# Packing the closing products of an attention-convolution kernel: 32 channels of o under c2's 96 rows, the other 64 as half pieces

## The chip, the cores and the metric

The kernel runs on one core of a Trainium2 chip. The time is the device time of one execution in microseconds (us); lower is better. Engines are named as in the profile: PE is TensorE's matmul queue and PEld its weight loads, DVE is VectorE, ACT is ScalarE, POOL is GpSimd, SP is SyncE, which here issues most DMAs.

## The reference, cut to what matters

Two layers work on x of 4 images, 96 channels, 128 x 128 pixels, float32. Layer 0 is a group norm, a projection with a depthwise convolution, a four-direction state-space scan and an output projection. Layer 1 is what matters here:

```python
xr, x1, x2 = _relu_split_norm(x, sc1, sc2, res_coef, nc1, nc2)
y1 = NORM_SCALE * _layer_norm(_attn_conv(x1, x2, aw1, aw2, aw3))
y2 = NORM_SCALE * _layer_norm(_conv2d(x2, w_conv2, K // 2)) * x1
y = jnp.concatenate([y1, y2], axis=1)
return xr + _conv2d(y, w_full, 0) + b_full[None, :, None, None]
```

`_attn_conv` convolves with weights that each image makes for itself by a softmax. Its output is called o below, and the convolution `_conv2d(x2, w_conv2)` is called c2. The last line is a 1 x 1 convolution over 2 x 96 channels: 96 of y1 and 96 of y2. The layer norms take one mean and one variance for a whole image. The kernel folds them in: o's scale `ro` goes into the weights, o's mean becomes a constant for each output channel, and c2 has its mean subtracted before it is multiplied by x1. `xr`, the residual, is piecewise linear in x with one slope and offset above a threshold and another below.

## The kernel before

The kernel is one instruction stream made by Python generators. `co_run(left, right, pace)` draws from two generators in turn; each `yield` tells how much time of the other side the piece is worth. After the scan of layer 0 (it ends near 3.4 ms), `left` is `attend` of image b: the image's convolutions by a product scheme with separate planes of pixels, first the two maps (c2 among them) and then the attention convolution that makes o. `light` is a chain of side work for the neighbouring images: `norm` and `split` of image b+1, then `close` of image b-1. A scheduler sets the final order of the instructions on every engine, and each engine then works through its queue in order.

Close is `attn_output`. It runs for images 0, 1 and 2, each time beside the attention of a later image. The last image is closed by another class, `LastOutput`, which uses `own_weights`, `c2_weights` and `residual` too but whose tile loop is not touched by the change.

Before its loop Close makes two weight matrices. `own_weights` (L2267 to L2274) makes `w1`: 96 rows of the 1 x 1 weights of o times `ro`, and a 97th row with the constants: `low`'s offset for each channel, less mean times weights, made by two small products (L2271, L2272). `c2_weights` makes `w2` (L2256). `with_ones` (L2278) makes two buffers for o whose 97th row is one, so that the product of `w1` with o adds the constant.

The loop goes over 16 tiles of 1024 pixels. For each tile:

- SP loads o, c2 and xx (the layer's input) of the next tile, 96 partitions x 4 KB each (L2312, L2315).
- `first_half`: ScalarE makes a linear function of xx (L2283) and VectorE masks it to x1 (L2284).
- VectorE subtracts c2's mean and multiplies by x1 (L2326), in place in `c2`.
- `residual`: ScalarE makes the upper branch's difference (L2288), VectorE masks it (L2289) and adds slope times xx (L2290).
- PE makes two results of 512 columns, one bank each, from two products each: `w1` with o (L2334), `w2` with c2 (L2335).
- VectorE adds the residual from `e` and evicts to `x1` (L2337 for image 0, whose maps have plain pixel order; L2339 for the others, which also reorders pixels).
- SP stores x1.

Tiles of pool `f3` have two buffers, and the bank pool of this side, `psr`, has two banks, so that at most one tile's results are open.

`ssm_output`, earlier in each image's life, has the same two-step packing for a product over 192 rows: 128 rows first (L1023), then 64 rows split in two halves of the pixels, which lie on partitions 0 to 63 and 64 to 127 (L1028).

Of the kernel before, what the change touches and what calls it, by code (L numbers as in the profile page):

```python
# [9 lines left out]
F32 = mybir.dt.float32  # L10
BF16 = mybir.dt.bfloat16
AF = mybir.ActivationFunctionType
ALU = mybir.AluOpType
# [4 lines left out]
C = 96  # L18
H = W = 128
L = H * W  # L20
CH = 512
# [32 lines left out]
SN = 1024  # L54
# [17 lines left out]
def kernel(  # L72
# [26 lines left out]
    nc = tc.nc  # L99
# [6 lines left out]
    def load(src, name):  # L106
        t = const.tile(list(src.shape), F32, name=name, tag=name)
        nc.sync.dma_start(t, src)
        return t
# [44 lines left out]
    def filled(value, name, n=C, p=C):  # L154
        t = const.tile([p, n], F32, name=name, tag=name)
        nc.vector.memset(t, value)
        return t

    mean96 = filled(1.0 / C, "mean96")
# [17 lines left out]
    def col(name, width=1, bufs=None):  # L177
        return small.tile([C, width], F32, name=name, tag=name, bufs=bufs)

    def rsqrt(dst, var):  # L180

        t = col("rsq")
        nc.vector.tensor_scalar(t, var, GN_EPS, None, ALU.add)
        nc.scalar.activation(t, t, AF.Sqrt)
        nc.vector.reciprocal(dst, t)

    def combine(ps, stats, mat, name, mv=None):


        if mv is None:  # L190
            mv = small.tile([stats.shape[0], 2], F32, name="mv", tag=f"mv{stats.shape[0]}")
            nc.vector.bn_aggr(mv, stats)  # L192
        n = mv.shape[0]
        p1 = bank(ps)[:n, 0:2]
        nc.tensor.matmul(p1, lhsT=mat, rhs=mv, start=True, stop=True)  # L195
        r = small.tile([n, 2], F32, name=name, tag=name)
        nc.vector.tensor_copy(r, p1)
        d2 = small.tile([n, 1], F32, name=f"d2{n}", tag=f"d2{n}")
        nc.vector.tensor_sub(d2, mv[:, 0:1], r[:, 0:1])
        nc.vector.tensor_mul(d2, d2, d2)  # L200
        p2 = bank(ps)[:n, 0:2]
        nc.tensor.matmul(p2[:, 0:1], lhsT=mat, rhs=d2, start=True, stop=True)  # L202
        nc.vector.tensor_add(r[:, 1:2], r[:, 1:2], p2[:, 0:1])
        return r, mv
# [84 lines left out]
    def bank(ps):  # L289

        return ps.tile([128, CH], F32, name="bank", tag="bank")

    def part(ps, *shape):
        n = 1
        for d in shape[1:]:
            n *= d
        t = bank(ps)[: shape[0], :n]
        return t if len(shape) == 2 else t.rearrange("p (a b) -> p a b", b=shape[2])
# [1922 lines left out]
            yield from lift(H)  # L2221
            later.flush()

    def c2_weights(img, ps, pool):


        n = NSTRIP
        mva, mvb = (pool.tile([128, 2], F32, name=f"mv_{i}") for i in "ab")
        for mv, st, p, e, k in (
            (mva, img.c2a, 96, 128, 4 * n - img.mapped),  # L2230
            (mvb, img.c2b, 0, 64, 2 * n - (not img.mapped)),
            (mvb, img.c2b, 64, 128, 2 * n - 1),
        ):
            v = st[p:e, :k].rearrange("p c s -> p (c s)")
            nc.vector.bn_aggr(mv[p:e], v)
        halves = ((mva[96:128], m96[96:128]), (mvb, mrows[img.mapped]))

        def over(n):
            pt = bank(ps)[:, 0:n]
            for i, (mv, mat) in enumerate(halves):  # L2240
                nc.tensor.matmul(
                    pt, lhsT=mat, rhs=mv[:, 0:n], start=(i == 0), stop=(i == 1)
                )
            return pt

        s2 = pool.tile([128, 2], F32, name="s2")
        nc.vector.tensor_copy(s2, over(2))
        for mv, p in ((mva, 96), (mvb, 0)):
            d = mv[p:128, 0:1]
            nc.vector.tensor_sub(d, d, s2[p:128, 0:1])  # L2250
            nc.vector.tensor_mul(d, d, d)
        nc.vector.tensor_add(s2[:, 1:2], s2[:, 1:2], over(1))
        r2 = col("r2")
        rsqrt(r2, s2[0:C, 1:2])
        w2 = pool.tile([C, C], F32, name="w2")
        nc.vector.tensor_scalar(w2, wful[:, 1], r2, None, ALU.mult)  # L2256
        return s2, w2

    def own_weights(img, ps, pool):

        so, _ = combine(ps, img.ost.rearrange("p c s -> p (c s)"), mean96, "so")
        ro = col("ro")
        rsqrt(ro, so[:, 1:2])
        w1 = pool.tile([128, C], F32, name="w1")
        nc.vector.tensor_scalar(w1[0:C], wful[:, 0], ro, None, ALU.mult)  # L2267
        nso = col("nso")
        nc.vector.tensor_scalar(nso, so[:, 0:1], -1.0, None, ALU.mult)
        pt = bank(ps)[C : C + 1, 0:C]  # L2270
        nc.tensor.matmul(pt, lhsT=img.keep["low"][:, 1:2], rhs=ident, start=True, stop=False)  # L2271
        nc.tensor.matmul(pt, lhsT=nso, rhs=w1[0:C], start=False, stop=True)  # L2272
        nc.vector.tensor_copy(w1[C : C + 1], pt)
        return w1[0 : C + 1]  # L2274

    def with_ones(pool, name, bufs=None):
        y = pool.tile([128, SN], F32, name=name, tag=name, bufs=bufs)
        nc.gpsimd.memset(y[C : C + 1], 1.0)  # L2278
        return y[0 : C + 1]

    def first_half(img, xx, x1):
        thr, scale, shift = (img.keep[n] for n in ("thr", "scale", "shift"))
        nc.scalar.activation(x1, xx, AF.Identity, scale=scale[:, 0:1], bias=shift[:, 0:1])  # L2283
        nc.vector.scalar_tensor_tensor(x1, xx, thr, x1, ALU.is_gt, ALU.mult)  # L2284

    def residual(img, xx, e):
        up, low, thr = (img.keep[n] for n in ("up", "low", "thr"))
        nc.scalar.activation(e, xx, AF.Identity, scale=up[:, 0:1], bias=up[:, 1:2])  # L2288
        nc.vector.scalar_tensor_tensor(e, xx, thr, e, ALU.is_gt, ALU.mult)  # L2289
        nc.vector.scalar_tensor_tensor(e, xx, low[:, 0:1], e, ALU.mult, ALU.add)  # L2290

    def pixels(v):

        return v.rearrange("p (h j t) -> p h t j", j=TW, t=TN)

    def plain(v):
        return v.rearrange("p (h t j) -> p h t j", j=TW, t=TN)

    def attn_output(img, ps, side, share):
        ob = out[img.b].rearrange("c h w -> c (h w)")  # L2300
        with (
            tc.tile_pool(name="f1", bufs=1, side=side) as p1,
            tc.tile_pool(name="f3", bufs=2, side=side) as p3,
        ):
            w1 = own_weights(img, ps, p1)
            s2, w2 = c2_weights(img, ps, p1)
            ones = [with_ones(p1, f"o{i}") for i in range(2)]

            def loads(t):
                o = ones[t % 2]  # L2310
                got = [o]
                nc.sync.dma_start(o[0:C], img.od[:, bass.ts(t, SN)])  # L2312
                for name, src in (("c2", img.c2d), ("xx", img.xnew)):
                    y = p3.tile([C, SN], F32, name=name)
                    nc.sync.dma_start(y, src[:, bass.ts(t, SN)])  # L2315
                    got.append(y)
                return got

            ahead = loads(0)
            for t in range(NS):  # L2320
                o, c2, xx = ahead
                if t + 1 < NS:
                    ahead = loads(t + 1)
                x1 = p3.tile([C, SN], F32, name="x1")
                first_half(img, xx, x1)
                nc.vector.scalar_tensor_tensor(  # L2326
                    c2, c2, s2[0:C, 0:1], x1, ALU.subtract, ALU.mult
                )
                e = p3.tile([C, SN], F32, name="e")
                residual(img, xx, e)  # L2330
                for h in range(2):
                    sl = bass.ts(h, CH)
                    pf = part(ps, C, CH)
                    nc.tensor.matmul(pf, lhsT=w1, rhs=o[:, sl], start=True, stop=False)  # L2334
                    nc.tensor.matmul(pf, lhsT=w2, rhs=c2[:, sl], start=False, stop=True)  # L2335
                    if img.mapped:
                        nc.vector.tensor_add(x1[:, sl], pf, e[:, sl])  # L2337
                    else:
                        nc.vector.tensor_add(plain(x1[:, sl]), pixels(pf), pixels(e[:, sl]))  # L2339
                    yield 2.6 * share  # L2340
                nc.sync.dma_start(ob[:, bass.ts(t, SN)], x1)

# [103 lines left out]
    class Image:  # L2446
# [44 lines left out]
        def close(self, ps, side, share=1.0):  # L2491
            while not self.finished:
                at.later.tick()
            yield from attn_output(self, ps, side, share)
# [27 lines left out]
    with tc.tile_pool(name="wp", bufs=1, side="left") as wp:  # L2522
# [7 lines left out]
        for images, pace in (([0], 0.25), ([1], 0.75), ([2, 3], 1.35)):  # L2530
            left = projections(images, weights, stats, wp, psl)
            if images[0] == 0:
# [12 lines left out]
                got = next(others)  # L2545
                while not got:
                    next(left)
                    got = next(others)
# [25 lines left out]
    wful = load(w_full, "wful")  # L2574
# [123 lines left out]
```

## Time and profile before

| what | us |
|---|---|
| median of 3 runs | 6410.42 (6406.12 to 6425.06) |
| the profiled execution | 6409.68 |
| its span, first to last instruction | 6407.8 |
| PE busy | 5253.4 (82% of the span) |
| DVE busy | 4699.9 (73%) |
| ACT busy | 3759.4 (59%) |
| POOL busy | 3238.6 (51%) |
| mean granted PE clock | 0.902 |

The page shows one execution. Busy times are shares of the whole span, averaged over stages that have different limits; what a part of the kernel costs has to be read from the stretch in which it runs. A row of a group gives line, engine, operation, tiles (out<-in), shapes and count, then busy time and mean duration, then the idle time of the engine just before and what ended it. Durations of neighbouring instructions on one engine overlap a little, so the busy time of a group, which counts overlap once, is smaller than count times mean. A float32 product of 512 columns leaves two PE records.

### The profile page before, as it was taken

To read this page: it belongs to the slowest core of one execution; us is meant where nothing else is said; L and a number is where in the kernel's file an instruction comes from. 1 tells how busy PE (TensorE), PEld (TensorE's weight loads), DVE (VectorE), ACT (ScalarE), POOL (GpSimd) and SP (SyncE) were. 2 spreads that over 40 slices of the span, in tenths; PEclk is the share of its full clock that TensorE was granted. 3 is DMA by queue.
4 is the path that set the end of the run, shared out by engine and by line. 5 is a ranking of instruction groups with operands and counts; after the bars stand their busy time and mean duration, and the time that the engine had idled before them with its cause. 6 is when DMAs were issued, how large, how long until landed. Compare 5 with 4: busy or idle time off the path is not lost. (4 is left out here: it accounts for less than half of the span.)

```text
span 6407.8 us, 76468 instructions
## 1 busy us (share of the span) xinstructions
PE 5253.4 (82%) x23264; PEld 2254.8 (35%) x23264; DVE 4699.9 (73%) x7132; ACT 3759.4 (59%) x4770; POOL 3238.6 (51%) x2476
## 2 busy tenths in 40 slices
PE   6889988987888643989988588977888877889888
PEld 2333322322222111444433234345333444345553
DVE  4247878988989768989844686468774687988767
ACT  1247767787787666777622465466644665545642
POOL 1326757978879554979822234436304365022310
PEclk9899989998999765999999799989989888999989
DMA  6766777775675766676667686665776656967668
GB/s 155 175 160 189 198 199 199 214 221 163 198 202 171 202 183 207 196 213 179 182 185 195 166 228 163 195 169 156 214 199 184 175 149 165 245 167 180 191 168 221
DMA packets 897706, 1205.30 MB, mean 188 GB/s; under 512 B 230644, under 2 KB 745642, under 8 KB 884816
## 3 DMA queue, kind: packets, MB, share of 16 engines
q1 hardware_dynamic: 866640, 1145.36, 65.5%
q0 software_dynamic: 16336, 38.51, 2.3%
q10 hardware_dynamic: 14320, 16.54, 0.9%
q8 instruction: 187, 3.06, 0.2%
q14 instruction: 223, 1.83, 0.1%
HBM read 777.82 MB, written 345.62 MB: 175 GB/s over the span
## 5 line engine op out<-in xcount | busy, mean ns | idle before, releaser
L633 PE MATMUL bank<-y,wp 128*128 128x512 f32 (+3 forms) x3584 | 1310.9, 622 | 83.8 <-DMA y<-y 41.0
L866 POOL TENSOR_TENSOR y<-y,dl 128x1024 f32<-128x1024 f32 x384 | 1058.5, 2757 | 263.0 <-DVE dl L858 240.3
L833 POOL TENSOR_TENSOR dl<-dl,u 128x1024 f32<-128x1024 f32 x384 | 1008.8, 2627 | 253.1 <-ACT dA L809 121.1
L854 DVE TENSOR_TENSOR_SCAN dA<-dA,pBC 128x512 f32<-128x512 f32 x768 | 981.6, 1278 | 30.7
L2169 PE MATMUL bank<-y,wn 128*64 128x384 f32 (+5 forms) x2408 | 680.1, 507 | 58.3 <-DMA y<-x1d 34.1
L1477 PE MATMUL two<-ya,wd 128*64 128x192 f32 (+3 forms) x2376 | 582.2, 414 | 174.0 <-ACT odd L1550 65.1
L633 PEld LDWEIGHTS bank<-y,wp 128*128 128x128 f32 (+3 forms) x3584 | 456.2, 168 | 749.3 <-issue 651.1
L858 DVE TENSOR_TENSOR dl<-dA,pBC 128x512 f32<-128x512 f32 x768 | 528.5, 688 | 255.8 <-PE pBC L747 183.8
L747 PE MATMUL pBC<-xr,wbc 60*128 60x512 bf16 (+1 forms) x1536 | 457.8, 404 | 311.5 <-DVE dA L854 239.1
L1938 ACT COPY yb<-ya 64x768 f32<-64x768 f32 (+1 forms) x660 | 537.7, 815 | 195.5 <-PE two L1477 113.8
L676 ACT ACTIVATE dl<-pd,dtb 128x512 f32<-128x512 f32 x768 | 485.5, 684 | 187.9 <-PE pd L747 171.5
L1477 PE MATMUL two<-yb,wd 128*64 128x192 f32 (+3 forms) x2376 | 559.0, 400 | 4.0 <-ACT yb L1938 4.0
L837 DVE TENSOR_TENSOR pBC<-dl,pBC 128x512 f32<-128x512 f32 x768 | 527.5, 687 | 8.8 <-POOL dl L833 7.8
L2169 PEld LDWEIGHTS bank<-y,wn 128*64 128x64 f32 (+3 forms) x2408 | 310.3, 169 | 357.2 <-issue 186.2
L809 ACT ACTIVATE dA<-dl,negA 128x1024 f32<-128x1024 f32 x384 | 420.3, 1141 | 2.3
L1477 PEld LDWEIGHTS two<-ya,wd 128*64 128x64 f32 (+1 forms) x2376 | 262.2, 165 | 370.9 <-ACT odd L1550 75.0
L676 ACT ACT_TABLE_LOAD x248 | 318.2, 1283 | 91.9 <-PE pd L747 79.7
L747 PEld LDWEIGHTS <-wbc 60*128 60x128 bf16 (+1 forms) x1536 | 103.1, 96 | 752.1 <-issue 739.3
L1477 PEld LDWEIGHTS two<-yb,wd 128*64 128x64 f32 (+1 forms) x2376 | 289.7, 167 | 150.5 <-issue 42.1
L1477 PE MATMUL two<-ya,wa 128*96 128x384 f32 (+1 forms) x528 | 231.2, 521 | 72.9 <-DMA ya<-vp 27.0
L1550 ACT COPY odd<-two 128x384 f32<-128x384 f32 (+5 forms) x176 | 115.8, 658 | 291.3 <-PE two L1492 179.1
L1406 POOL TENSOR_TENSOR pl<-x 96x256 f32<-96x256 f32 (+3 forms) x396 | 275.2, 710 | 0.0
(322 smaller groups left out, 9105.4 us busy)
## 6 DMA issues: line engine op xcount, KB each, us to landing
u<-zb SPq DMA_DIRECT2D x192, 1024.0 KB
yms<-y SPq DMA_DIRECT2D x96, 512.0 KB
xn<-xnew SPq DMA_DIRECT2D x128, 384.0 KB
ya<-vp SPq DMA_DIRECT2D x120, 336.0 KB
y<-y SPq DMA_DIRECT2D x128, 258.2 KB
zb<-z SPq DMA_DIRECT2D x64, 512.0 KB
y<-yms SPq DMA_DIRECT2D x64, 512.0 KB
ya<-x1p SPq DMA_DIRECT2D x90, 336.0 KB
```

Of the source, the lines that this page charges most:

```text
L633: nc.tensor.matmul(blocks(pz[p:e]), lhsT=ws[k][:, d, c : c + e - p], rhs=window(ys[k], at, d, n), start=(i == 0), stop=(i == len(terms) - 1),)
L676: nc.scalar.activation(dst, src, AF.Softplus, bias=bias)
L747: nc.tensor.matmul(p, lhsT=w[rows], rhs=xr[rows, at : at + CH], start=True, stop=True)
L809: nc.scalar.activation(live[m]["dA"], live[m]["dl"], AF.Exp, scale=negA[:, g % 3, k : k + 1])
L833: nc.gpsimd.tensor_mul(t, t, u_view(n))
L837: nc.vector.tensor_mul(p, live[n]["dl"][:, bass.ts(half, CH)], p)
L854: nc.vector.tensor_tensor_scan(h, h, p, init, ALU.mult, ALU.add)
L858: nc.vector.tensor_mul(live[n]["dl"][:, sl], live[n]["dA"][:, sl], live[n]["C", half])
L866: nc.gpsimd.tensor_add(v, v, t.rearrange("p (a b) -> p a b", b=W))
L1477: nc.tensor.matmul(of(to[p:e], r), lhsT=w[:, i, c : c + e - p], rhs=tiles(t[k][PAIR[i]][:, SLOT[i]], o, r), start=(k == 0), stop=False,)
L1938: nc.scalar.copy(yb[k][64 * h - 64 : 64 * h, :, :n], ya[k][0:64, :, h * TN : h * TN + n])
L2169: nc.tensor.matmul(pc[p:e, :n].rearrange("p (h w) -> p h w", w=W), lhsT=w[:, c : c + e - p], rhs=v[:, :, 0:W], start=(i == 0), stop=(i == ...
```

## The change

Close is rewritten so that its rows fill the array. Of o's 96 channels, the first 32 are loaded under c2's 96 rows, so that one product contracts 128 rows with the stacked weights `stack[:, 0]`. The other 64 channels are loaded in two pieces of 512 pixels, one on partitions 0 to 63 and one on 64 to 127, and multiplied by `stack[:, 1]`, which holds the same 64 weight rows twice. The row of ones goes. Its constant, now a column `base` from a product of one column, is the bias of a ScalarE operation that makes slope times xx plus base in its own tile `g`; VectorE adds `g` to `e`. Both banks of a tile are taken before its products. A tile has five loads in place of three. The weights `w2` are written straight into the stack and `w1`'s rows are copied into it by three DMAs on POOL's queue. `own_weights` is split, so that `LastOutput` keeps what it had.

```diff
--- before.py
+++ after.py
@@ -2221,7 +2221,7 @@
             yield from lift(H)
             later.flush()
 
-    def c2_weights(img, ps, pool):
+    def c2_weights(img, ps, pool, w2=None):
 
 
         n = NSTRIP
@@ -2252,21 +2252,24 @@
         nc.vector.tensor_add(s2[:, 1:2], s2[:, 1:2], over(1))
         r2 = col("r2")
         rsqrt(r2, s2[0:C, 1:2])
-        w2 = pool.tile([C, C], F32, name="w2")
+        if w2 is None:
+            w2 = pool.tile([C, C], F32, name="w2")
         nc.vector.tensor_scalar(w2, wful[:, 1], r2, None, ALU.mult)
         return s2, w2
 
+    def own_scale(img, ps):
+
+        so, _ = combine(ps, img.ost.rearrange("p c s -> p (c s)"), mean96, "so")
+        ro, nso = col("ro"), col("nso")
+        rsqrt(ro, so[:, 1:2])
+        nc.vector.tensor_scalar(nso, so[:, 0:1], -1.0, None, ALU.mult)
+        return ro, nso
+
     def own_weights(img, ps, pool):
 
-
-
-        so, _ = combine(ps, img.ost.rearrange("p c s -> p (c s)"), mean96, "so")
-        ro = col("ro")
-        rsqrt(ro, so[:, 1:2])
+        ro, nso = own_scale(img, ps)
         w1 = pool.tile([128, C], F32, name="w1")
         nc.vector.tensor_scalar(w1[0:C], wful[:, 0], ro, None, ALU.mult)
-        nso = col("nso")
-        nc.vector.tensor_scalar(nso, so[:, 0:1], -1.0, None, ALU.mult)
         pt = bank(ps)[C : C + 1, 0:C]
         nc.tensor.matmul(pt, lhsT=img.keep["low"][:, 1:2], rhs=ident, start=True, stop=False)
         nc.tensor.matmul(pt, lhsT=nso, rhs=w1[0:C], start=False, stop=True)
@@ -2302,41 +2305,67 @@
             tc.tile_pool(name="f1", bufs=1, side=side) as p1,
             tc.tile_pool(name="f3", bufs=2, side=side) as p3,
         ):
-            w1 = own_weights(img, ps, p1)
-            s2, w2 = c2_weights(img, ps, p1)
-            ones = [with_ones(p1, f"o{i}") for i in range(2)]
+            ro, nso = own_scale(img, ps)
+            w1 = p1.tile([C, C], F32, name="w1")
+            nc.vector.tensor_scalar(w1, wful[:, 0], ro, None, ALU.mult)
+            pt = bank(ps)[:C, 0:1]
+            nc.tensor.matmul(pt, lhsT=w1, rhs=nso, start=True, stop=True)
+            base = col("base")
+            nc.vector.tensor_add(base, pt, img.keep["low"][:, 1:2])
+            stack = p1.tile([128, 2, C], F32, name="ws")
+            s2, _ = c2_weights(img, ps, p1, stack[0:C, 0])
+            nc.gpsimd.dma_start(stack[C:128, 0], w1[0:32])
+            for h in range(2):
+                nc.gpsimd.dma_start(stack[64 * h : 64 * h + 64, 1], w1[32:C])
 
             def loads(t):
-                o = ones[t % 2]
-                got = [o]
-                nc.sync.dma_start(o[0:C], img.od[:, bass.ts(t, SN)])
-                for name, src in (("c2", img.c2d), ("xx", img.xnew)):
-                    y = p3.tile([C, SN], F32, name=name)
-                    nc.sync.dma_start(y, src[:, bass.ts(t, SN)])
-                    got.append(y)
-                return got
+                c2 = p3.tile([128, SN], F32, name="c2")
+                o = p3.tile([128, CH], F32, name="o")
+                xx = p3.tile([C, SN], F32, name="xx")
+                nc.sync.dma_start(c2[0:C], img.c2d[:, bass.ts(t, SN)])
+                nc.sync.dma_start(c2[C:128], img.od[0:32, bass.ts(t, SN)])
+                nc.sync.dma_start(xx, img.xnew[:, bass.ts(t, SN)])
+                for h in range(2):
+                    nc.sync.dma_start(
+                        o[64 * h : 64 * h + 64], img.od[32:C, bass.ts(2 * t + h, CH)]
+                    )
+                return o, c2, xx
 
             ahead = loads(0)
+            up, low, thr = (img.keep[n] for n in ("up", "low", "thr"))
             for t in range(NS):
                 o, c2, xx = ahead
                 if t + 1 < NS:
                     ahead = loads(t + 1)
                 x1 = p3.tile([C, SN], F32, name="x1")
                 first_half(img, xx, x1)
+                d = c2[0:C]
                 nc.vector.scalar_tensor_tensor(
-                    c2, c2, s2[0:C, 0:1], x1, ALU.subtract, ALU.mult
+                    d, d, s2[0:C, 0:1], x1, ALU.subtract, ALU.mult
                 )
                 e = p3.tile([C, SN], F32, name="e")
-                residual(img, xx, e)
+                nc.scalar.activation(e, xx, AF.Identity, scale=up[:, 0:1], bias=up[:, 1:2])
+                g = p3.tile([C, SN], F32, name="g")
+                nc.scalar.activation(g, xx, AF.Identity, scale=low[:, 0:1], bias=base)
+                nc.vector.scalar_tensor_tensor(e, xx, thr, e, ALU.is_gt, ALU.mult)
+                nc.vector.tensor_add(e, e, g)
+                pf = [part(ps, C, CH) for _ in range(2)]
+                for h in range(2):
+                    nc.tensor.matmul(
+                        pf[h], lhsT=stack[:, 0], rhs=c2[:, bass.ts(h, CH)],
+                        start=True, stop=False,
+                    )
+                for h in range(2):
+                    p = slice(64 * h, 64 * h + 64)
+                    nc.tensor.matmul(
+                        pf[h], lhsT=stack[p, 1], rhs=o[p], start=False, stop=True
+                    )
                 for h in range(2):
                     sl = bass.ts(h, CH)
-                    pf = part(ps, C, CH)
-                    nc.tensor.matmul(pf, lhsT=w1, rhs=o[:, sl], start=True, stop=False)
-                    nc.tensor.matmul(pf, lhsT=w2, rhs=c2[:, sl], start=False, stop=True)
                     if img.mapped:
-                        nc.vector.tensor_add(x1[:, sl], pf, e[:, sl])
+                        nc.vector.tensor_add(x1[:, sl], pf[h], e[:, sl])
                     else:
-                        nc.vector.tensor_add(plain(x1[:, sl]), pixels(pf), pixels(e[:, sl]))
+                        nc.vector.tensor_add(plain(x1[:, sl]), pixels(pf[h]), pixels(e[:, sl]))
                     yield 2.6 * share
                 nc.sync.dma_start(ob[:, bass.ts(t, SN)], x1)
 
```

In the changed program the lines are: L2287 for x1's mask, L2343 for c2's operation, L2347 and L2349 for ScalarE's two operations, L2350 and L2351 for the mask and the add, L2354 for the two products of 128 rows, L2360 for the two half products, L2366 (image 0) and L2368 for the evictions.

## The prediction

> **What bounds the kernel now.** The page's first part gives TensorE (PE) 82% of the span and VectorE (DVE) 73%. Its chain covers about 1% and settles nothing, so I went by stage. The changed function, Close, runs three times (close 0, 1, 2, for images 0 to 2). The groups by form from 4640 us on, and the starts of L2334 and L2335, put them at 4646 to 4778, 5450 to 5660 and 5660 to 5906 us. The table of stretches for these (columns: busy us of PE, PEld, DVE, ACT, POOL, then granted PE clock, DMA share, GB/s):
>
> ```profile
> core 0: us, PE busy (x) PEld busy (x) DVE busy (x) ACT busy (x) POOL busy (x), PEclk, DMA share, GB/s
> 4646.00:4778.00 132.00, 105.09 (x290) 38.45 (x287) 112.55 (x127) 50.96 (x50) 13.71 (x13) 0.82 0.70 195
> 5450.00:5605.00 155.00, 138.20 (x420) 55.58 (x419) 141.96 (x178) 83.22 (x95) 0.00 (x0) 0.97 0.92 245
> 5605.00:5660.00 55.00, 46.92 (x187) 22.55 (x186) 44.19 (x69) 21.52 (x27) 2.83 (x5) 0.87 0.61 164
> 5660.00:5906.00 246.00, 224.14 (x1269) 119.69 (x1267) 200.18 (x283) 117.02 (x142) 74.81 (x94) 0.96 0.68 177
> ```
>
> The reader is to see three different limits. Close 0 is VectorE's (112.6 of 132 us). Close 1's first 155 us are tight everywhere: DVE 92%, DMA 92% at 245 GB/s, PE 89%. Close 2 is PE's (91%, DVE 81%, DMA 68%). Then the operations concerned, with out<-in, shapes, count, busy us, mean ns and the idle time before them:
>
> ```profile
> L2335 PE MATMUL bank<-c,w 96*96 96x512 f32 x192 | 108.2, 691 | 21.7 <-DVE c L2326 18.7 <-issue 2.7
> L2334 PE MATMUL bank<-o,w 97*96 97x512 f32 x192 | 105.5, 670 | 6.2 <-DVE x L2337 5.7 <-DVE x L2339 0.3
> L1023 PE MATMUL bank<-y,outws 128*96 128x512 f32 x64 | 34.7, 658 | 0.0
> L1028 PE MATMUL bank<-yr,outws 64*96 64x512 f32 x64 | 22.0, 628 | 0.0
> L2290 DVE SCALAR_TENSOR_TENSOR e<-xx,kept,e 96x1024 f32<-96x1024 f32 x64 | 85.7, 1340 | 0.2
> L2440 DVE TENSOR_TENSOR e<-two,e 96x1024 f32<-96x1024 f32 x16 | 19.5, 1221 | 12.9 <-PE two L2436 12.9
> L2288 ACT ACTIVATE e<-xx,kept 96x1024 f32<-96x1024 f32 x64 | 78.6, 1230 | 27.7 <-DMA xx<-xnew 19.1 <-DVE x L2337 6.5 <-DVE x L2284 2.1
> ```
>
> An f32 product of 512 columns is two records, so 192 records are 96 products. L1023 and L1028 already do in `ssm_output` what the change does in Close: L1023 contracts 128 rows, L1028 sends 64-row halves to the two partition halves. Its busy time, 22.0 us, is about half of 64 x 628 ns = 40.2 us: the halves run side by side. Last, VectorE's waits (total us, times, longest) in close 0 and in 5440 to 5660:
>
> ```profile
> DVE x L2337 <- PE bank L2335: 9.6, 13, 1.9
> ...
> DVE x L2339 <- PE bank L2335: 14.5, 10, 3.4
> ```
>
> In close 2 it is 6.4 us. VectorE's queue is in order, so such a wait stops all its later work, attention's too.
>
> [...] on the timeline at 5021 us the four L1023 records start 1.88 us ahead of the L1028 ones, which take 1.04 us until the next matmul. [...] L2440 shows 1221[...]; L2288 shows 1230. [...] four L2335 records take 1.88 us at 4684 and 3.73 at 4758, and close 0's clock is 0.82.
>
> **The change, part by part (48 tiles, 16 a close).**
>
> *TensorE.* Per tile four products become two of 128 rows (same price: L1023's 34.7/64 = 0.54 us a record, L2335's 108.2/192 = 0.56) and two half ones. The 192 o records fall from 105.5 us to 192 x 22.0/64 = 66.0: **-39.5 us of PE**, 13.2 a close. Weight loads lie under the matmuls. The bias row and its products (L2271, two records of 96 columns) become one column: under 1 us a close.
>
> *The order.* This is the cost. Before, o's products needed no VectorE result and ran ahead; after c's operation (L2326) only c's two products remained, and the first eviction could start some 1.0 us after it. Now both c products stand first and wait for it (L2343), the halves follow, and both banks are ready after 1.9 + 1.1 + 0.2 = 3.2 us. What covers this is what VectorE does between c's operation and the first eviction in its own order. Counting both programs' VectorE orders at the trace's starts-to-starts (1.19 us for an operation of 1024, 0.6 for an eviction in close 0, 1.0 in the others, about 0.58 for one of attention's), the cover before falls short of 1.2 us by 0.1 us in all; in the changed order it falls short of 3.2 us by **11 us in close 0, 16 in close 1, 9 in close 2**. That is new waiting if PE comes at once; it is less where PE is late anyhow, which the 14.5 us of close 1 show, and PE now reaches c's products 1.9 us of o work earlier. Range: 0 to 36 us over the three; I take half where VectorE is the limit (6 + 7 us) and nothing in close 2, where it has 46 us of idle time.
>
> *VectorE's operations.* L2290 becomes a plain add[...], 48 x 0.05 = -2 us, at most 48 x 0.12 = -6.
>
> *ScalarE.* One more operation of 1.23 us a tile: 48 x 1.23 = 59 us, 20 a close. ScalarE is 39%, 54% and 48% busy there, so the work fits; queued behind it are attention's evictions (L1550) and `yb` copies, for which PE waits. Close 2 shows under 8 us of such PE waits on L1550; I charge +2 us in each of closes 1 and 2, from 0 to 10 in all.
>
> *DMA and SP.* The bytes are equal: 4 x 384 KB a tile. Two more issues a tile at L2312's median 0.37 us: 0.75 us of SP in 8 to 15 us a tile. They stand last, after xx, so c, its o rows and xx are issued as before, and attention's loads behind them come 0.7 us later, two strips ahead of use: 0, and 5 us if that lead is gone. In the trace's packet times of close 1, 4 KB took 235 ns and packets near 2 KB (1792 B) 116, a few per cent more a byte for 1/6 of the traffic: +1 us in close 1.
>
> *Setup.* The three copies into `ws` go through POOL. [...] in close 0 w1 is ready at 4602 us and the first c product is at 4651, in close 2 5660 and 5677, so they are hidden[...]. The memsets of ones (2 x 0.95 us a close on POOL) go; nobody waited for them but the next close's buffers.
>
> *Moved attention work.* The PE order of close 0 keeps 24 of attention's products fewer ahead of its last tile (54 after the first tile against 78 before). At about 0.4 us each that is 10 us of PE that VectorE's time no longer covers. Behind close 0 PE is full for 20 us, then 81%: +4, bounds 0 and 10.
>
> **The sum.** Close 0: +6 (waits) +4 (moved) -1 (add) = +9; PE's 13.2 us gain little there, since VectorE sets the pace. Close 1: +7 +2 +1 -1, and PE and the first 155 us's DMA give back about half of 13.2: +3. Close 2: -13.2 x 0.9 + 2 = -10. Together about **+2 us** on the profiled execution's 6409.7, which lies 0.7 under the median of the runs: 6412 us.
>
> **Rivals.**
>
> *PE's gain comes through (faster).* For it: PE is 89% and 91% busy in closes 1 and 2, and in close 0's half-clock stretches the o and c products together take up to 7.4 us a tile, as long as the tile itself. If the new waits hide behind PE's lateness, three quarters of 39.5 us come out: 6410 - 30 + 2 = **6382 us**. Against it: 92% DMA share in close 1, VectorE in close 0.
>
> *VectorE stalls on the late banks (slower).* One mechanism: the evictions L2366 and L2368 wait in order for products that begin only after L2343. It decides where VectorE is the limit and the cover is under 3.2 us, from about half of the shortage on. In full, closes 0 and 1 pay 11 + 16 us; in close 0, whose PE queue holds twelve tiles in a row with no attention product between them (43% busy at 3 us of 7), the half clock lengthens 3 us to near 6 and adds about 10. With +4 (moved work), +3 (ScalarE and DMA in close 1), -2 (adds), -7 (PE in close 1) and -10 (close 2): 6410 + 25 = **6435 us**. Against it: PE was often the late one in close 1.
>
> *The halves do not overlap*, so that the change doesn't do what it says: 192 half records at full price. Then the 12 + 7 us that PE gave back in closes 2 and 1 are missing, and each bank comes 0.9 us later, some 10 us over the tiles with short cover: 6412 + 19 + 10 = 6441 us. L1028 speaks against it; it lies inside the slower case.
>
> **How the numbers follow.** 0.3%, 19 us, is about what a measurement of this kernel can tell from no change. Balance 0.38, PE's gain 0.27, VectorE's stall 0.35. The first case is the likeliest, with its own range of 6393 to 6429. For the range to hold 8 in 10 it must reach into both others: 6374 (PE's 39.5 us nearly whole) to 6452 (all the waits, the clock and the bounds of ScalarE and setup).
>
> **What would show it.** Right: the o records (L2360) near 66 us of PE busy time for 192; VectorE's waits for `bank` in the closes up from 30.5 us to 45 to 65; L2349 48 times at 1.23 us; L2351 near 1.22. Close 2 shorter than 246 us by about 10, close 0 not shorter than 132. Wrong: L2360 above 90 us (no overlap); VectorE's waits unchanged and close 1 shorter (the faster rival); or the difference lying in 4800 to 5440 or behind 5906, where only the order of other work moves.

## The result, and the profile after

The changed kernel is **slower by 0.8%**: 6467.22 us in the median of 6 runs (6445.67 to 6474.66) against 6409.98 us of 6 runs before; the ratio is 1.0077, with a 95% interval from 1.0057 to 1.0096. The prediction had 6412 us with a range that ended at 6452, so the result lies outside. The profiled execution took 6445.67 us, its span is 6443.9 us. It is the fastest of its six, and it reaches Close 25 us earlier than the trace before does (ScalarE's first operation of close 0 starts at 4620.5 us against 4645.6), in work that the two kernels share. From that operation to the end of VectorE's last operation it takes 61.5 us more: this is what has to be explained.

The closes as stretches, with the columns of the table before (the stretch and its length, busy us of PE, PEld, DVE, ACT, POOL, then PE clock, DMA share, GB/s):

```profile
4621.00:4767.00 146.00, 94.11 (x285) 30.26 (x286) 114.24 (x132) 68.51 (x66) 7.26 (x14) 0.77 0.69 189
5435.00:5610.00 175.00, 140.34 (x415) 50.50 (x414) 136.34 (x172) 96.48 (x106) 0.00 (x0) 0.87 0.79 207
5610.00:5662.00 52.00, 39.88 (x182) 17.80 (x180) 42.86 (x58) 26.07 (x31) 1.00 (x3) 0.93 0.65 177
5662.00:5932.00 270.00, 237.39 (x1401) 125.70 (x1400) 212.23 (x323) 141.02 (x168) 65.21 (x99) 0.93 0.64 167
```

All three closes are longer, and no engine is clearly fuller for it, except ScalarE, which has one operation more a tile. Close 1's first part had three resources at 89 to 92%; now VectorE is at 78%, PE at 80%, DMA at 79%. Nothing has become the bound: everything waits more. The groups by form (busy us, mean ns of one, then the idle time before and what ended it):

```profile
L2354 PE MATMUL bank<-c,ws 128*96 128x512 f32 x192 | 133.0, 831 | 98.9 <-DVE c L2343 71.3 <-issue 26.0 <-DVE x L2366 0.8
...
L2286 ACT ACTIVATE x<-xx,kept 96x1024 f32<-96x1024 f32 x64 | 79.3, 1240 | 73.3 <-DMA xx<-xnew 62.1 <-DMA out<-x 10.7 <-issue 0.3
...
L2360 PE MATMUL bank<-o,ws 64*96 64x512 f32 x192 | 64.8, 758 | 0.0
...
L2351 DVE TENSOR_TENSOR e<-e,g 96x1024 f32<-96x1024 f32 x48 | 60.4, 1262 | 0.3
...
L2349 ACT ACTIVATE g<-xx,base,kept 96x1024 f32<-96x1024 f32 x48 | 58.4, 1227 | 0.4 <-DMA xx<-xnew 0.4
```

The half products overlap as forecast: 64.8 us of PE for 192 records. But the stacked products take 831 ns a record where L2335 took 691; the run "c not awaited" below shows that this comes with the wait ahead of them. In this trace from 5700 to 5800 us a tile's four such records took 1.96 us at a granted clock of 1.00 where PE had stood idle for 0.17 to 0.39 us (three tiles), and 3.50 to 3.70 us at 0.50 to 0.54, the half clock, where it had stood idle for 0.97 to 4.98 us (three tiles). PE's waits for L2343 are long (71.3 us; for L2326 before, 18.7), VectorE's waits for the banks have doubled (65.4 us against 30.5), and so nearly have ScalarE's for xx (67.7 against 36.1). Of the banks, images 1 and 2 before and after:

```profile
L2339 DVE TENSOR_TENSOR x<-bank,e 96x512 f32<-96x512 f32 x64 | 64.8, 1036 | 21.5 <-PE bank L2335 20.9
```

```profile
L2368 DVE TENSOR_TENSOR x<-bank,e 96x512 f32<-96x512 f32 x64 | 64.6, 1040 | 47.6 <-PE bank L2360 47.5
```

By stretches, first VectorE's waits in close 0 (4621 to 4767; total us, times, longest):

```profile
DVE x L2287 <- ACT x L2286: 19.2, 4, 8.8
DVE x L2366 <- PE bank L2360: 17.9, 11, 5.8
```

and in close 1 (5435 to 5662):

```profile
DVE x L2368 <- PE bank L2360: 29.7, 13, 4.7
DVE x L2287 <- ACT x L2286: 12.6, 5, 4.3
```

Two chains of waits end in these lines: the bank, late behind the c operation (L2343), and the first half's operation (L2286), late behind the load of xx. ScalarE's own waits in close 0 show the second one. Before:

```profile
ACT e L2288 <- DMA xx<-xnew: 16.3, 4, 4.7
...
ACT x L2283 <- DMA xx<-xnew: 6.6, 3, 2.9
```

After:

```profile
ACT x L2286 <- DMA xx<-xnew: 39.5, 7, 9.2
...
ACT e L2347 <- DMA xx<-xnew: 5.2, 1, 5.2
```

Each chain could be the cause and the other its symptom, because they close a loop over two tiles: eviction, store, load of xx for the tile after the next, L2286, L2287, L2343, products, eviction. Experiments have to cut it.

To see where a kernel loses, I use the same four marks of the timeline in every trace: from ScalarE's first x<-xx of close 0 to the last L970 product of the norm behind it (A); from the first x<-xx of close 1 to the last `wa` product of the attention beside it (B); from there to LastOutput's first x<-xx (C); from there to the end of VectorE's last operation (D). Before they are 359.1, 157.9, 304.6 and 483.1 us; after, A is 13.1 us longer, B 26.3, C 14.8, D 9.9. There is one trace of each kernel, and the split between C and D shifts easily: with three loads, o last, C is 18.2 us shorter and D 21.2 longer. The table has the runs that decide, in us against before (what lies between A and B, within 5 us in these, is left out):

| kernel | A | B | C | D |
|---|---|---|---|---|
| changed | +13.1 | +26.3 | +14.8 | +9.9 |
| changed, c not awaited | +12.4 | +12.4 | +4.6 | +6.5 |
| changed, o's loads on POOL | +13.4 | -3.0 | +3.2 | +6.3 |
| changed, that and three buffers | -6.2 | -0.4 | +3.6 | +13.9 |
| before, five loads in the old order | +33.3 | +31.4 | +21.2 | +4.1 |
| before, two tiny loads on SP | +14.3 | +26.7 | +16.4 | +9.4 |
| before, two tiny loads on POOL | -2.5 | +0.1 | -3.4 | +1.3 |

### The profile page after: what moved, and what is told of

Read it like the earlier page. It is cut to its first block, busy times and chain, and to the rows that moved or that the text cites. A ratio compares the mean times of both kernels' runs of the same rounds, so it can differ in the third digit from the quotient of the medians.

```text
span 6443.9 us, 76635 instructions
## 1 busy us (share of the span) xinstructions
PE 5249.4 (81%) x23258; PEld 2239.0 (35%) x23258; DVE 4689.6 (73%) x7132; ACT 3812.7 (59%) x4818; POOL 3213.7 (50%) x2479
## 5 line engine op out<-in xcount | busy, mean ns | idle before, releaser
L1477 PEld LDWEIGHTS two<-yb,wd 128*64 128x64 f32 (+1 forms) x2376 | 289.8, 169 | 156.2 <-issue 38.1
```

Source lines behind the costliest of these rows:

```text
L1477: nc.tensor.matmul(of(to[p:e], r), lhsT=w[:, i, c : c + e - p], rhs=tiles(t[k][PAIR[i]][:, SLOT[i]], o, r), start=(k == 0), stop=False,)
```

## The experiments

An eviction is VectorE's read of a finished bank. The edits are shortened: arguments are cut, and loops and loads are written in words where that is plainer. Theories: **1**, the order of the products (PE waits for L2343 with nothing to run ahead, at half clock, and the banks are late); **2**, the loads (late xx, by the number or the order of five loads); **3**, the added ScalarE operation; **4**, both banks taken and finished together. Each ratio is to runs of the kernel before on the same chip, with its 95% interval; a distance in us is the ratio less one, times 6410 us. The changed kernel's is 49 us in this count (37 to 62). Three kernels, "c not awaited", "old residual" and "xx early and c not awaited", leave part of the result out, as their forecasts say.

### First: order, wait, ScalarE operation

**Halves first.** The two half products stand ahead of the stacked ones:

```diff
-  for h in range(2): matmul(pf[h], stack[:, 0], c2[:, bass.ts(h, CH)], start=True, stop=False)
   for h in range(2): matmul(pf[h], stack[p, 1], o[p], ...)
+  for h in range(2): matmul(pf[h], stack[:, 0], c2[:, bass.ts(h, CH)], start=False, stop=True)
```

> The changed kernel with the two half products of o issued first and the two stacked products last; everything else as changed. Theory 1 (order: both stacked products stand first and wait for VectorE's c operation L2343, PE has no o work to run ahead with, so the banks come 3 us after it and PE drops to half clock): most of the loss goes, 6385 to 6415 us, VectorE's waits for the banks in the closes fall from 65 us to below 40. Theory 2 (the xx loads come late) and theory 3 (the added ScalarE operation): no change to speak of, 6450 to 6467 us, and VectorE's waits for ScalarE's L2286 (57.6 us) stay above 45.

Measured: 6482.01 us, ratio 1.0145 (1.0123 to 1.0167). Giving PE its work ahead made it worse. VectorE's waits for the banks fell from 65.4 to 54.8 us only, and ScalarE's for xx ahead of L2286 stay at 58.9 us (62.1 after). Why it is slower than the change is open.

**c not awaited.**

```diff
-  d = c2[0:C]
-  scalar_tensor_tensor(d, d, s2, x1, subtract, mult)
+  d = p3.tile([C, SN], F32, name="d", bufs=1)
+  scalar_tensor_tensor(d, c2[0:C], s2, x1, subtract, mult)
```

> The changed kernel with the c operation writing a tile of its own that nobody reads, so that the stacked products read c2 as loaded (the mean's subtraction and the product with x1 are missing in the output) and PE no longer waits for L2343; order, loads and ScalarE work as changed. Theory 1 (the wait for L2343 and its half clock): 6385 to 6420 us, PE's idle time ahead of the stacked products falls from 98.9 us to below 40. Theories 2 (late xx loads) and 3 (added ScalarE operation): 6445 to 6467 us.

Measured: 6424.79 us, ratio 1.0061 (1.0044 to 1.0078). By form, from 4615 us on:

```profile
L2354 PE MATMUL bank<-c,ws 128*96 128x512 f32 x192 | 107.3, 687 | 38.1 <-DVE x L2366 36.2 <-issue 1.7 <-DMA c<-od 0.2
L2287 DVE SCALAR_TENSOR_TENSOR x<-xx,kept,x 96x1024 f32<-96x1024 f32 x64 | 84.0, 1312 | 77.5 <-ACT x L2286 77.2
```

The wait for L2343, and with it the slow records, is gone: idle time falls from 98.9 to 38.1 us, a record from 831 to 687 ns. Yet the ratio's interval overlaps the changed kernel's. VectorE's idle time before L2287 rose from 57.8 us (after) to 77.5: the late load takes over part of what the banks gave up. Theory 1 alone is a part at most.

**Old residual**, in the changed kernel:

```diff
-  activation(e, xx, Identity, scale=up[:, 0:1], bias=up[:, 1:2])
-  g = p3.tile([C, SN], F32, name="g")
-  activation(g, xx, Identity, scale=low[:, 0:1], bias=base)
-  scalar_tensor_tensor(e, xx, thr, e, is_gt, mult)
-  tensor_add(e, e, g)
+  residual(img, xx, e)
```

> The changed kernel with the old residual: no g tile, no added ScalarE operation, VectorE adds slope times xx again; the constant column base is left out of the output. Theory 3 (the ScalarE operation delays the evictions of attention and the first half's operation behind it): 6410 to 6435 us. Theory 1 (order and late banks) and theory 2 (late loads): 6450 to 6467 us.

Measured: 6448.09 us, ratio 1.0095 (1.0080 to 1.0110): nothing is gained. Theory 3 falls as the main cause.

**The ScalarE operation alone**, in the kernel before:

```diff
-  scalar_tensor_tensor(e, xx, low[:, 0:1], e, mult, add)
+  g = p3.tile([C, SN], F32, name="g")
+  activation(g, xx, AF.Copy, scale=low[:, 0:1])
+  tensor_add(e, e, g)
```

> The kernel before with the residual alone done in the new way: a ScalarE copy with scale into its own tile g (no bias, the constant stays in the row of ones) and a plain VectorE add; unpacked products, three loads. Theory 3: 6435 us or more. Theories 1 and 2: 6405 to 6420 us, no difference that can be told.

Measured: 6404.93 us, ratio 1.0020 (1.0006 to 1.0033): 4 to 21 us, 13 in the middle, below the 0.3% that the prediction takes for no change.

### Second: the loads in parts

**xx early**, in the changed kernel:

```diff
-  xx = p3.tile([C, SN], F32, name="xx")
-  load c2[0:C]; load c2[C:128]; load xx; load o's halves
+  xx = p3.tile([C, SN], F32, name="xx", bufs=3)
+  load xx; load c2[0:C]; load c2[C:128]; load o's halves
```

> The changed kernel with xx loaded first of a tile's five loads and into three buffers, so that it never waits for the tile before the last; products, order and ScalarE work as changed. Theory 2 (late xx loads, issued behind c2's and o's rows and the store): the distance to the kernel before falls from 49-57 us to 10-30 us and VectorE's waits for ScalarE's L2286 fall below 20 us. Theory 1 (only the wait of the stacked products for L2343): 45 to 60 us stay.

Measured: 6460.24 us, ratio 1.0072 (1.0048 to 1.0096): no gain. ScalarE's waits for xx fell from 62.1 to 42.3 us only: the load stands in SP's order behind the store and c2's rows of earlier tiles all the same.

**Five loads alone.** The kernel before, unpacked, with the changed kernel's loads:

```diff
-  sync.dma_start(o[0:C], od[:, bass.ts(t, SN)]); c2; xx
+  sync.dma_start(c2, ...); sync.dma_start(o[0:32], od[0:32, bass.ts(t, SN)]); sync.dma_start(xx, ...)
+  for h in range(2):
+      sync.dma_start(o[32:C, bass.ts(h, CH)], od[32:C, bass.ts(2 * t + h, CH)])
```

> The kernel before with five loads a tile in the changed kernel's order (c2, o's first 32 rows, xx, two column pieces of o's other 64 rows, in place on o's 96 partitions); products, order and residual as before. Theory 2 in its strict form (the number and order of loads alone): 15 to 30 us slower than before. Theory 1, and theory 2 in the form that the loads are late only because the store ahead of them waits for later evictions: within 8 us of before.

Measured: 6490.46 us, ratio 1.0116 (1.0079 to 1.0154). This is the turn: the loads by themselves cost as much as the whole change, or more. ScalarE's waits in its close 0:

```profile
ACT x L2283 <- DMA xx<-xnew: 65.9, 12, 8.1
```

against 6.6 us on that line before, and 16.3 on L2288. My expectation of 15 to 30 us was far too low.

**xx early and c not awaited**: the kernel of xx early, with

```diff
-  scalar_tensor_tensor(d, d, s2, x1, subtract, mult)
+  scalar_tensor_tensor(x1, c2[0:C], s2, x1, subtract, mult)
```

> The kernel of the early xx with the c operation writing into x1, so that the stacked products read c2 as loaded (output without the mean's subtraction and the product with x1). If theories 1 and 2 together are the whole loss: 25 us faster than before to 5 us slower. If there is a third cause (the order in which attention's products stand between those of Close): 10 to 30 us slower.

Measured: 6420.39 us, ratio 1.0019 (1.0008 to 1.0029). With the loop cut at two places most of the loss goes, although either cut alone gave little: against xx early, on the same chip, the wait for L2343 is now worth 34 us. SP still has all five loads here and the kernel is 12 us over before, so what five loads cost depends on the waits that stand beside them.

**Bank by bank.** The changed kernel's products in the order of the kernel before:

```diff
-  pf = [part(ps, C, CH) for _ in range(2)]; both stacked products; both half products; both evictions
+  for h in range(2):
+      pf = part(ps, C, CH)
+      matmul(pf, stack[p, 1], o[p], start=True, stop=False)
+      matmul(pf, stack[:, 0], c2[:, sl], start=False, stop=True)
+      evict pf to x1[:, sl]
```

> The changed kernel with the products in the order of the kernel before: for each half a bank, the half product of o, the stacked product, the eviction; loads and ScalarE work as changed. Theory 4 (both banks taken and finished together is what makes the evictions late): the distance to before falls from 49-57 us to 0-25 us. Theory 2 (loads): 45 us or more stay. In the kernel with both half products first, 94 us were measured.

Measured: 6490.91 us, ratio 1.0120 (1.0091 to 1.0149). Theory 4 falls. With the old order of products the packed kernel costs what five loads cost unpacked (1.0116): the packing then gives nothing back. The order that the change chose gives back some 0.4%, by intervals that overlap a little.

### Third: number, order or queue

**Five loads in the old order**, in the kernel before:

```diff
-  load o[0:C]; load c2; load xx
+  load o[0:32]; load o[32:C, 0:CH]; load o[32:C, CH:SN]; load c2; load xx
```

> The kernel before with five loads a tile, but o's three pieces first and then c2 and xx, as the kernel before has them. If the number of loads on SP's queue is what costs: 50 us or more over before, as the five loads in the changed kernel's order did (72 to 85 us). If only the order counts (o's pieces behind xx, c2 ahead of it): 0 to 20 us.

Measured: 6490.57 us, ratio 1.0118 (1.0101 to 1.0135): the number counts.

**Three loads, o last**, in the kernel before:

```diff
-  load o[0:C]; load c2; load xx
+  load c2; load xx; load o[0:C]
```

> The kernel before with its three loads in the order c2, xx, o. If the order of the loads is what costs: 40 us or more over before. If the number of loads on SP's queue is: 0 to 20 us.

Measured: 6419.51 us, ratio 1.0018 (1.0009 to 1.0027): the order costs 6 to 17 us, not 76.

**Store on POOL**, in the changed kernel:

```diff
-  nc.sync.dma_start(ob[:, bass.ts(t, SN)], x1)
+  nc.gpsimd.dma_start(ob[:, bass.ts(t, SN)], x1)
```

> The changed kernel with the store of x1 issued from POOL's queue instead of SP's, so that the loads of the tile after the next no longer stand behind a store that waits for this tile's evictions. If the loop eviction, store, load of xx, first half, c operation, products is what sets a tile's time: at most 20 us over before, SP's waits for the evictions gone and close 0 shorter than 142 us. If the issue time of five loads by itself costs: 40 us or more stay.

Measured: 6443.85 us, ratio 1.0041 (1.0025 to 1.0057), 26 us over before: between the two forecasts, half the loss.

**o's loads on POOL**, in the changed kernel:

```diff
-  nc.sync.dma_start(c2[C:128], img.od[0:32, ...]); for h: nc.sync.dma_start(o[64*h : 64*h + 64], ...)
+  nc.gpsimd.dma_start(c2[C:128], img.od[0:32, ...]); for h: nc.gpsimd.dma_start(o[64*h : 64*h + 64], ...)
```

> The changed kernel with the three loads of o's rows on POOL's queue, so that SP issues c2, xx and the store alone; packing, products and ScalarE work as changed. If the loads on SP's queue are the cause (number or order): -20 to +15 us against before. If the late banks of the stacked products are: 35 us or more over before.

Measured: 6430.23 us, ratio 1.0027 (1.0017 to 1.0037), 17 us over before: about two thirds of the loss go. B, 26.3 us longer after, is 3.0 us shorter than before here, with the packed products and their order unchanged. VectorE's waits for the banks are back to 33.0 us, near the 30.5 before; for images 1 and 2:

```profile
L2368 DVE TENSOR_TENSOR x<-bank,e 96x512 f32<-96x512 f32 x64 | 65.5, 1041 | 22.9 <-PE bank L2360 22.5
```

So most of the lateness of the banks came from the loads, and not from the order of the products. A, close 0 and the norm behind it, is as long as in the changed kernel.

### Fourth: issues or bytes

**Two tiny loads** in the kernel before, behind each tile's three:

```diff
+  for h in range(2):
+      z = p3.tile([C, 8], F32, name=f"z{h}")
+      nc.sync.dma_start(z, img.od[:, bass.ts(128 * t + h, 8)])
```

> The kernel before with two loads of 96 x 32 bytes added behind each tile's three, into tiles that nobody reads. If the issues on SP's queue are what costs: 40 us or more over before. If it is the pieces and packet sizes of the real loads: 0 to 15 us.

Measured: 6470.25 us, ratio 1.0103 (1.0080 to 1.0127). Loads of 3 KB that nobody reads cost 66 us on this queue. In the table its four stretches are the changed kernel's to within 2 us: the change loses its time where two more issues on SP alone lose it.

**Four loads.** o's halves in one load of 128 partitions:

```diff
-  for h in range(2): sync.dma_start(o[64*h : 64*h + 64], od[32:C, bass.ts(2 * t + h, CH)])
+  sync.dma_start(o, od[32:C, bass.ts(t, SN)].rearrange("c (h n) -> h c n", h=2))
```

> The changed kernel with o's two halves in one load over all 128 partitions (four loads a tile, all on SP). If the number of loads costs: between the changed kernel's 49 to 57 us and the 17 us with o's loads off SP, so 20 to 40 us over before. If the pieces' packets (2 KB, unchanged here) cost: 45 us or more.

Measured: 6497.10 us, ratio 1.0138 (1.0119 to 1.0158): one load fewer, and 88 us over before. **Two o loads on POOL** is the kernel with o's loads on POOL, with the same merged load:

```diff
-  for h in range(2): nc.gpsimd.dma_start(o[64*h : 64*h + 64], ...)
+  nc.gpsimd.dma_start(o, od[32:C, bass.ts(t, SN)].rearrange("c (h n) -> h c n", h=2))
```

> The changed kernel with o's halves in one load and both loads of o on POOL's queue. If issues cost on POOL too: 0 to 12 us over before, less than the 17 us with three. If what remains there is the late banks and the added ScalarE operation: 14 to 25 us.

Measured: 6499.72 us, ratio 1.0140 (1.0116 to 1.0163). Both forecasts failed, so this dose says nothing of the number. The DMA view of POOL's issues from 4640 to 5950 (count, KB each, median us to landing) with three loads:

```profile
o<-od POOLq DMA_DIRECT2D x96, 128.0 KB, 4.7
```

and with the merged one:

```profile
o<-od POOLq DMA_DIRECT2D x45, 256.0 KB, 11.8
```

The merged load lands 7 us later, so it is another, slower transfer. POOL's queue also has more packets with it in this stretch (29,450 against 9,408); the cause stays open.

**o on POOL in the kernel before**, the control for that queue:

```diff
-  nc.sync.dma_start(o[0:C], img.od[:, bass.ts(t, SN)])
+  nc.gpsimd.dma_start(o[0:C], img.od[:, bass.ts(t, SN)])
```

> The kernel before with its load of o on POOL's queue, nothing else changed. If SP's queue is short in the kernel before too: 5 to 20 us faster than before. If it has enough room there: within 8 us.

Measured: 6397.85 us, ratio 0.9983 (0.9969 to 0.9997): 2 to 20 us faster, 11 in the middle, again below 0.3%.

### Fifth: the queue, and a candidate

**Tiny loads on POOL**:

```diff
-      nc.sync.dma_start(z, img.od[:, bass.ts(128 * t + h, 8)])
+      nc.gpsimd.dma_start(z, img.od[:, bass.ts(128 * t + h, 8)])
```

> The kernel before with the same two loads of 96 x 32 bytes a tile, but on POOL's queue; the order of PE, VectorE, ScalarE and SP is then that of the kernel before. If SP's queue is what costs 60 us with them on SP: within 10 us of before. If two more transfers of any queue cost it: 40 us or more.

Measured: 6404.38 us, ratio 0.9996 (0.9983 to 1.0009). The same transfers cost nothing from another queue. What SP does with the difference shows in its waits in close 2 (from the first x<-xx, 245 us). The kernel before and the one with the tiny loads on POOL:

```profile
SPq L1921 <- PE two L1492: 46.4, 7, 10.2
```

```profile
SPq L1921 <- PE two L1492: 42.4, 7, 10.2
```

With the tiny loads on SP this wait has shrunk to

```profile
SPq L1921 <- PE two L1492: 0.8, 1, 0.8
```

L1921 loads attention's strips. Before, SP stands ready and waits for PE to free the strip's buffer, so the load leaves at the first moment possible. With the two loads more SP mostly comes there after the buffer is free. This shows where SP's lead went and not what it costs: with o's load on POOL in the kernel before the wait is 15.2 us, and that kernel is no slower. The queue is late though it is far from full: in the first 145 us of close 0 SP of the kernel before issues 83 DMAs in 34 us together.

**The candidate**, o's loads on POOL and

```diff
-  c2 = p3.tile([128, SN], F32, name="c2"); o = p3.tile([128, CH], F32, name="o")
+  c2 = p3.tile([128, SN], F32, name="c2", bufs=3); o = p3.tile([128, CH], F32, name="o", bufs=3)
```

> The changed kernel with the three loads of o's rows on POOL's queue, and c2 and o in three buffers, so that POOL's loads wait less for the products of the tile before the last. If that wait (60 us of POOL's time in close 0) is the rest of the loss: -25 to +5 us against before. If the rest lies in the products' order and the added ScalarE operation: 10 to 25 us over before.

Measured: 6413.09 us, ratio 1.0012 (0.9999 to 1.0025): as fast as before, not faster. POOL's waits for L2354 in close 0 fell only from 59.7 to 54.8 us, so the mechanism I gave it is not confirmed, although A is now 6.2 us shorter than before. No version here beats the kernel before by 0.3%.

## Why the prediction was wrong

**The step that failed is "DMA and SP"**: "Two more issues a tile at L2312's median 0.37 us: 0.75 us of SP in 8 to 15 us a tile ... attention's loads behind them come 0.7 us later, two strips ahead of use: 0, and 5 us if that lead is gone." Added to the kernel before, it measured 66 us (two tiny loads) to 76 us (five loads), and nothing for the tiny loads on another queue; taken from SP in the changed kernel, o's loads give back 32 us. What then remains, 17 us, or 8 with three buffers, lies inside the range of the prediction: this one term puts the result outside it. I compared issue time with the tile's time, as if SP were an engine with room. What I left out is that its queue is in order and that most of its time is waiting: some 106 of the first 145 us of close 0 before. In the changed kernel's SP timeline in close 0 the o loads at 4696.54 us stand behind a store that waited until 4696.1 for L2366, though the products that read o's buffer (L2360) had ended by 4694.8 (start us, us, line, operation):

```profile
4692.88 0.31 SPq L2325 DMA_DIRECT2D c<-c2d  x1
4693.24 0.42 SPq L2326 DMA_DIRECT2D c<-od  x1
4696.13 0.32 SPq L2370 DMA_DIRECT2D out<-x  x1
4696.54 1.15 SPq L2329 DMA_DIRECT2D o<-od  x2
4700.45 0.31 SPq L2325 DMA_DIRECT2D c<-c2d  x1
4700.81 0.42 SPq L2326 DMA_DIRECT2D c<-od  x1
4701.34 0.36 SPq L2327 DMA_DIRECT2D xx<-xnew  x1
```

and the kernel before's:

```profile
4714.73 0.30 SPq L2315 DMA_DIRECT2D xx<-xnew  x1
4716.59 0.30 SPq L2315 DMA_DIRECT2D c<-c2d  x1
4717.31 0.32 SPq L2341 DMA_DIRECT2D out<-x  x1
4720.27 0.30 SPq L2312 DMA_DIRECT2D o<-od  x1
```

The five issues take 0.31 + 0.42 + 0.36 + 1.15 = 2.2 us where three took 0.9, so 1.3 us more and not 0.75, and between them stand a store that waits for this tile's evictions and a c2 load that waits for its products. SP's waits for the evictions at the store in close 0, before (4646 to 4791) and after (4621 to 4767):

```profile
SPq L2341 <- DVE x L2337: 29.5, 14, 10.1
```

```profile
SPq L2370 <- DVE x L2366: 40.5, 16, 5.9
```

I said "c, its o rows and xx are issued as before"; they are not. An issue takes 0.3 to 0.6 us in the lines above, but two more of them a tile on SP cost 66 us here, with the order of the instructions that came with them.

Two parts of this cost are not separated: the issues themselves at run time, and the order of all engines, which the scheduler writes anew. With the tiny loads on POOL the orders of PE, VectorE, ScalarE and SP are the kernel before's; with them on SP they are not. In close 0 the store then often stands directly ahead of the loads of c2 and xx, and SP waits there 48.9 us for evictions against 29.5 before. Three loads in another order also changed the orders of all engines and cost 12 us, and o on POOL in the kernel before changed them and gained 11; this speaks against order alone, but no run kept the order and added the issues on SP.

The other steps:

- *TensorE*, -39.5 us: L2360 was priced right (66.0 forecast, 64.8 measured). But L2354 grew from L2335's 108.2 to 133.0 us, so PE's busy time in Close fell by 15.9 us only. The prediction's sum had no slow records; the half clock stood in the slower rival alone.
- *The order*: the number fits by luck. "11 us in close 0, 16 in close 1, 9 in close 2" sum to 36; the trace has 65.4 us of waits for the bank against 30.5, 35 more. But with o's loads on POOL and the same order of products they are 33.0 us, and the two tiny loads alone raise them to 47.0 in the kernel before; so most of these waits are the loads' doing. That such a wait stops VectorE's later work shows in close 1 before: the attention's L1572 at 5581.0 us stood behind a wait of 2.8 us for L2335 and the evictions that followed it, though VectorE had written its inputs by 5563.3. By itself the wait for L2343 is worth 10 us, by overlapping intervals; with xx early it is worth 34. The two causes work through one loop and don't add.
- *ScalarE*: 48 operations of 1.23 us as forecast; its +4 lies at the lower end of the 4 to 21 us of the operation alone, which include VectorE's add (a mean of 1262 ns in the changed kernel, against 1221 for L2440's add before).
- *VectorE's operations*, -2: an estimate, 48 times the 0.05 us between L2290's median (1275 ns) and L2440's add (1221). The means are 1340 ns for L2290 before and 1262 for L2351 after.
- *Close 2*, -10: C became 14.8 us longer. With SP relieved (o's loads on POOL) it is still 3.2 longer: PE's freed time has not come out in the total of any packed kernel.
- *Moved attention work* and *Setup* were not tried by themselves. That the copies into `ws` are hidden was an estimate; in the trace after they landed 1.6 to 6.2 us after issue in close 0, 2.0 to 2.4 in close 1 and 3.8 to 5.4 in close 2, at least 9 us ahead of the first stacked product of their close.
- *The rivals*: "VectorE stalls on the late banks" had the right direction, slower, and the wrong cause. The sign I named for it, 45 to 65 us of waits, appeared. A sign that two causes share proves neither.

## What to carry to other kernels

Price an added DMA by its place in its queue, not by its issue time alone (two tiny loads a tile cost 66 us on SP's queue, and on POOL's the ratio was 0.9996): ask which store or load with a wait stands beside it, and what lies behind, other stages' loads included. Where waits form a loop over tiles, removing the longest one can move it to the next (with c not awaited, VectorE's idle time before L2287 rose from 57.8 to 77.5 us); add the suspected cost alone to the old kernel, as the two tiny loads did here, before trusting the new kernel's waits. Before rows are split to fill an array, count what the split adds to the queue that feeds it: five loads in place of three cost 74 to 76 us here.

## What the runs showed that I had not expected

- Two loads of 3 KB a tile, 96 in all, cost 1.03% on SP's queue and nothing (0.9996) on POOL's.
- One merged load over 128 partitions landed after 11.8 us where each of the two halves took 4.7 (on POOL's queue), and the kernels with it were 1.4% slower than before on either queue.
- Issuing o's products ahead of the wait, to which the prediction's account of the order points as the remedy, was slower than the change: 1.0145.
